# Blocks 4 to 7 of x: turned by DMA and VectorE instead of TensorE in the first pass of a graph layer

## The chip, the cores and the metric

The kernel runs on one core of one Trainium2 chip, in float32. The metric is the device time of one execution in microseconds; lower is better. Times within a profile are microseconds from the start of its span. TensorE (PE, with its weight loads PEld), VectorE (DVE), ScalarE (ACT), GpSimd (POOL) and SyncE (SP, which here issues most DMAs) each work through their own instructions in order.

## The reference

One layer on x of 4096 rows by 256, with a weighted adjacency of 4096 by 4096:

```python
def _layernorm(x, axis=-1, eps=1e-5):
    m = jnp.mean(x, axis=axis, keepdims=True)
    v = jnp.var(x, axis=axis, keepdims=True)
    return (x - m) / jnp.sqrt(v + eps)
...
    def _L0_gnn_ref(features, adj, neigh_W, lin_W):
        h = features @ neigh_W.T
        deg = adj.sum(axis=1, keepdims=True) + 1.0
        h = adj @ h / deg
        z = jnp.concatenate([features, h], axis=-1) @ lin_W.T
        return z
...
    x = x + _L0_gnn_ref(_layernorm(x, axis=-1), adj, L0_gnn_neigh_W, L0_gnn_lin_W)
    x = x + _L0_ffn_ref((_layernorm(x, axis=-1))[None], ...)[0]
```

The second half, causal attention over the 4096 rows and eight experts of which each row takes two, comes after all that is spoken of here.

## The kernel before

x is held as 8 blocks of 512 rows, `res[b]`, each of 4 tiles of 128 rows. The graph half is `adj` times the normed x (`g`), pass by pass: `aggregate(b, steps)` makes the rows of block b and runs over jb = 0 to 7, the blocks of neighbours. One (b, jb) is called a step. It takes seven products of half-size matrices (a Strassen-like scheme, L538) from the adjacency block `a` (1 MB, three buffers, loaded by SyncE three steps ahead at the end of each step, L278), from sums of its quarters, and from the normed block `g[jb]` and its differences. The sums are made by `halve(n)` on VectorE (L495 to L498).

The program is written under a manual schedule: each engine's instructions run in the order in which the code issues them. Work is put in by hand: after the fourth product of a step, the functions in `steps[jb]` are issued; after the seventh those of `steps[jb, "end"]`; then `load(...)`; then `steps[jb, "loaded"]`.

The first pass (b = 0) also prepares x, in functions that take a block:

- `scales_x`: mean and variance on VectorE (`bn_stats` L159, `bn_aggr` L161), then rstd on GpSimd in two operations (L165, L166).
- `normed_x`: VectorE norms a tile into `g[b]` (L451); the four of block b+1 are issued at the head of `features(b)`.
- `turned_x`: TensorE turns the normed block, 8 transposes of 128x128 (L437), and ScalarE copies them out of PSUM into `qT[b % 4]` (L439).
- `features`: TensorE multiplies the turned block by the first half of lin_W, 8 matmuls (L509), and VectorE adds the result onto `res[b]` (L514).
- `halve_x`: a small copy of ones into a column of `g[b]` (ScalarE, L463; that column gives the degrees), then VectorE makes four differences (L467 to L470), which read the ones.

In step jb the list is halve(jb+1), features(jb+2), halve_x(jb+2), scales_x(jb+4), and at its end turned_x(jb+3). Blocks 0 and 1 are done ahead of the first step, and turned_x(2) in step 0. In step 3 `load_rest` issues the loads of the attention's weights.

In the later passes `qkv(b - 1)` puts the projections of the block finished before into the steps. It has another way to turn a block: `norm` puts the normed rows, in an order of columns grouped by 32, into `kT[b]` and `vv[b]` (not yet used for their own ends); `leave` stores these in a DRAM tile `turning` (L599, two DMAs); `fetch` brings them back so that every 32x32 square lies where it belongs (L611, four DMAs, runs of 256 bytes); `turn` turns the squares on VectorE (L621, two instructions).

Of the kernel before, what the change touches and what calls it, by code (L numbers as in the profile page):

```python
# [9 lines left out]
F32 = mybir.dt.float32  # L10
I32 = mybir.dt.int32
SP = mybir.EngineType.SP
AF = mybir.ActivationFunctionType
ALU = mybir.AluOpType
# [3 lines left out]
P = 128  # L18
N = 4096
C = 256  # L20
NB = 8
TB = 4
# [9 lines left out]
Q = HD // 2  # L32
# [34 lines left out]
def fast_kernel(  # L67
# [24 lines left out]
    nc = tc.nc  # L92
# [13 lines left out]
    ones = const.tile([P, P], F32, name="ones")  # L106
# [13 lines left out]
    for e in range(NE):  # L120
# [16 lines left out]
    res = [  # L137
        res_all[:, b * TB * C : (b + 1) * TB * C].rearrange("p (t c) -> p t c", t=TB)
        for b in range(NB)
    ]  # L140
    qT_all = const.tile([P, NB * 2 * 512], F32, name="qT_all")
# [4 lines left out]
    mv = [const.tile([P, TB, 2], F32, name=f"mv{b}") for b in range(NB)]  # L146
# [42 lines left out]
    def in_order(x):  # L189
        return x.rearrange("p (g c d) -> p c g d", g=4, c=2)  # L190

    def in_groups(x):
        return x.rearrange("p (c g d) -> p c g d", g=4, c=2)
# [65 lines left out]
    with (  # L259
# [161 lines left out]
        HC = C // 2  # L421
# [17 lines left out]
                nc.scalar.copy(dst[:, :, cols], tr.rearrange("p c t i -> p c (t i)"))  # L439

        turned = {}

        def scales_x(b, at_a_time=TB):
            for t in range(0, TB, at_a_time):
                some = slice(t, t + at_a_time)
                stats(gx, b, range(TB)[some])
                power(rstd[b][:, some], mv[b][:, some, 1:2], 1.0, EPS_LN)

        def normed_x(b, t):
# [3 lines left out]
                mv[b][:, t, 0:1], rstd[b][:, t], op0=ALU.subtract, op1=ALU.mult,  # L453
            )

        def turned_x(b):

            turned[b] = qT[b % 4]
            transposed(lambda t, c: g[b][:, t // 2 * 2 + c, t % 2, :], turned[b])

        def halve_x(b):

            nc.scalar.copy(  # L463
                g[b][:, 1:4:2, :, HC - 1], ones[:, 0:4].rearrange("p (k t) -> p k t", k=2)
            )
            part = [g[b][:, k] for k in range(7)]
            nc.vector.tensor_sub(part[T1], part[G12], part[G11])  # L467
            nc.vector.tensor_sub(part[T3], part[G22], part[G12])
            nc.vector.tensor_sub(part[T2], part[G22], part[T1])
            nc.vector.tensor_sub(part[T4], part[T2], part[G21])  # L470
# [28 lines left out]
            halves_of[n] = m  # L499
        def features(b):  # L500
            fT = turned.pop(b)
            for t in range(TB if b + 1 < NB else 0):
                normed_x(b + 1, t)
            for h in range(2):
                pj = p_pj.tile([P, 2, C], F32, tag="pj", name=f"pf_{b}_{h}")
                for t in range(2):
                    for c in range(2):
                        at = (2 * h + t) * P
                        nc.tensor.matmul(  # L509
                            pj[:, t, :], fT[:, c, at : at + P], l1_sb[:, c, :],  # L510
                            start=(c == 0), stop=(c == 1),
                        )
                x1 = res[b][:, 2 * h : 2 * h + 2, :]
                nc.vector.tensor_add(x1, x1, pj)  # L514
# [52 lines left out]
                ),  # L567
            )

        turning = [tc.dram_tile([512, C], F32, name=f"turning{n}") for n in range(2)]  # L570
        last_z = gs.tile([P, 1024], F32, name="last_z")

        def qkv(b):

            made = {}

            def scales():
                stats(gx, b)
                var = mv[b][:, :, 1:2]
                power(both[b], var, *BOTH)  # L580
                power(rstd[b], var, 1.0, EPS_LN)

            def norm():

                made["h0"] = [
                    t.rearrange("p (t c) -> p t c", t=2)
                    for t in (kT[b], vv[b].rearrange("p t c -> p (t c)"))
                ]
                for t in range(TB):
                    nc.vector.tensor_scalar(  # L590
                        in_order(made["h0"][t // 2][:, t % 2, :]), in_groups(res[b][:, t, :]),
                        mv[b][:, t, 0:1], both[b][:, t], op0=ALU.subtract, op1=ALU.mult,
                    )
                made["ratio"] = ratio(gx, b)

            def leave():

                for n, h0 in enumerate(made.pop("h0")):
                    nc.sync.dma_start(  # L599
                        turning[b % 2][n * 2 * P : (n + 1) * 2 * P].rearrange(  # L600
                            "(t p) c -> p t c", p=P
                        ),
                        h0,
                    )

            def fetch():

                made["z"] = qT_all[:, (b + 1) * 1024 : (b + 2) * 1024] if b + 2 < NB else last_z
                squares = turning[b % 2].rearrange("(m i) (g e) -> g i m e", i=Q, g=4)
                for n in range(4):  # L610
                    nc.sync.dma_start(  # L611
                        made["z"][n * Q : (n + 1) * Q].rearrange("p (m e) -> p m e", e=2 * Q),
                        squares[n],
                    )

            def turn():

                made["hT"] = qT[b]
                z = made.pop("z").rearrange("p (m c d) -> p c m d", c=2, d=Q)
                for c in range(2):  # L620
                    nc.vector.transpose(  # L621
                        qT[b][:, c, :].rearrange("p (m i) -> p m i", i=Q), z[:, c]
                    )

            def values_and_logits():
                for h in range(2):
                    pj = p_tr.tile([P, 2, 2, P], F32, tag="tr", name=f"pv_{b}_{h}")
                    pj = pj.rearrange("p c t i -> p c (t i)")
                    for i in range(2):
                        at = (2 * h + i) * P  # L630
                        for c in range(2):
                            nc.tensor.matmul(  # L632
                                pj[:, i, 0 : NE + P], made["hT"][:, c, at : at + P],
                                wqkv_sb[:, c, QK:], start=(c == 0), stop=(c == 1),
                            )
                    nc.scalar.copy(vv[b][:, 2 * h : 2 * h + 2, :], pj[:, :, NE : NE + P])  # L636
                    for i in range(2):
                        t = 2 * h + i
                        nc.scalar.activation(
                            first_lg[b][:, t, :], pj[:, i, 0:NE], AF.Copy,  # L640
                            scale=made["ratio"][:, t],
                        )

            def turned_heads(ms):
                pjs = [p_pj.tile([P, 512], F32, tag="pj", name=f"pq_{b}_{m}") for m in ms]
                for m, pj in zip(ms, pjs):
                    for c in range(2):
                        nc.tensor.matmul(
                            pj, wqkv_sb[:, c, m * P : (m + 1) * P], made["hT"][:, c, :],
                            start=(c == 0), stop=(c == 1),  # L650
                        )
                for m, pj in zip(ms, pjs):
                    to = kT[b] if m == 2 else qT[b][:, m, :]
                    rot = gx.tile([P, 512], F32, tag="rot", name=f"rot_{b}_{m}", bufs=1)
                    nc.vector.tensor_mul(to, pj, tables[b][:, 0, :])  # L655
                    for n in range(4):
                        nc.scalar.activation(  # L657
                            rot[n * Q : (n + 1) * Q, :], pj[(n ^ 1) * Q : ((n ^ 1) + 1) * Q, :],
                            AF.Copy, scale=1.0 if n % 2 else -1.0,
                        )  # L660
                    nc.gpsimd.tensor_mul(rot, rot, tables[b][:, 1, :])  # L661
                    nc.gpsimd.tensor_add(to, to, rot)

            return [
                [scales, lambda: turn_tables(b)], [norm, leave], [],
                [values_and_logits, lambda: turned_heads((2,))], [lambda: turned_heads((0, 1))],
            ], {
                (2, "end"): [fetch], (2, "loaded"): [lambda: spread_tables(b)],
                (3, "end"): [turn],
            }  # L670
# [26 lines left out]
        steps = {jb: [] for jb in range(NB)}  # L697
        for jb in range(NB):
            for f, b in (
                (halve, jb + 1), (features, jb + 2), (halve_x, jb + 2), (scales_x, jb + 4),  # L700
            ):
                if b < NB or f is halve:
                    steps[jb].append(lambda f=f, b=b: f(b))
            if jb + 3 < NB:
                steps[jb, "end"] = [lambda b=jb + 3: turned_x(b)]
        steps[0].insert(1, lambda: turned_x(2))
        steps[3].append(load_rest)
        for jb, f in ((5, scale_rest), (6, bounds), (6, turn_wo), (7, router_wo)):
# [2117 lines left out]
```

## Time and profile before

| | us |
|---|---|
| median of 3 runs | 1512.12 (1512.09 to 1512.35) |
| the profiled execution, its own time | 1511.47 |
| its span, first to last instruction | 1509.8 |
| ahead of the first step | 0 to 18.46 |
| first pass, step 0 | 18.46 to 30.41 |
| steps 1 to 4, each | 10.37 or 10.38 |
| step 5 | 71.90 to 81.28 |

| instruction (mean in the first pass) | ns |
|---|---|
| transpose on TensorE, record, 128x128 (L437) | 276 |
| copy of 128x512 out of PSUM on ScalarE (L439) | 588 |
| norm of a tile of 128x256 on VectorE (L451) | 408 |
| `bn_stats` of a tile (L159) | 412 |
| square transposes of 128x512 on VectorE (L621) | 691 |
| copy of ones on ScalarE (L463) | 209 |

A line of the order of time gives start, length, engine and line of the kernel, operation, output and input, how many were merged, and in brackets for how long the engine was idle before it and what ended that. A line of the busy times by stage gives the stretch, its length, then for PE, PEld, DVE, ACT and POOL busy microseconds and instructions, then the granted TensorE clock (1 is full), the share of the DMA engines and GB/s. Records of matmuls overlap, so a group's cost is read from starts, not from the sum of records.

### The profile page before, as it was taken

How to read it: one execution, taken by the hardware profiler on the slowest of the kernel's cores; microseconds unless marked ns; L12 is line 12 of the kernel's file. 1: busy time of each engine (PE TensorE's matmuls, PEld its weight loads, DVE VectorE, ACT ScalarE, POOL GpSimd, SP SyncE). 2: the span in 40 equal slices, each digit the busy share in tenths (PEclk: the TensorE clock that was granted, in tenths of full speed). 3: DMA queues.
4: the chain of work that ended last, by engine and by line, in shares of the span. 5: the costliest groups of instructions: out<-in, count | busy, mean ns of one | idle time of the engine just before them, and what ended most of it. 6: DMA issues, size and time to landing. Idle time of an engine off the chain costs nothing. (4 is left out here: it accounts for less than half of the span.)

```text
span 1509.8 us, 28585 instructions
## 1 busy us (share of the span) xinstructions
PE 1496.9 (99%) x10731; PEld 1102.8 (73%) x10731; DVE 1083.9 (72%) x2239; ACT 544.9 (36%) x975; POOL 568.9 (38%) x649
## 2 busy tenths in 40 slices
PE   9999999999999999999999999999999999999997
PEld 7888888888888544444444444358899999999996
DVE  7855666656765577779879879795676877777872
ACT  2102011021020455655665655653222334343341
POOL 2102122121221331374565553551523464554542
PEclk9999999999999999999999999999999999999999
DMA  7435645555566000011010110029977898999965
GB/s 244 133 119 178 201 147 173 166 170 171 162 184 185 21 15 22 24 59 30 30 59 28 36 41 30 30 87 336 251 180 225 254 278 233 264 272 246 270 155 135
DMA packets 127005, 220.56 MB, mean 146 GB/s; under 512 B 79530, under 2 KB 103338, under 8 KB 113226
## 3 DMA queue, kind: packets, MB, share of 16 engines
q1 hardware_dynamic: 113322, 200.39, 42.3%
q0 software_dynamic: 12720, 17.47, 6.6%
q8 instruction: 86, 1.41, 0.4%
q10 hardware_dynamic: 816, 0.79, 0.2%
q14 instruction: 61, 0.50, 0.1%
HBM read 188.67 MB, written 31.33 MB: 146 GB/s over the span
## 5 line engine op out<-in xcount | busy, mean ns | idle before, releaser
L826 PE MATMUL sc<-qT_all,kT 64*64 64x512 f32 (+3 forms) x2304 | 282.1, 557 | 0.5 <-ACT pt_all L834 0.3
L538 PE MATMUL acc<-a,g 128*128 128x256 f32 x1024 | 244.0, 379 | 0.0
L538 PEld LDWEIGHTS acc<-a,g 128*128 128x128 f32 x1024 | 194.1, 190 | 32.2 <-issue 6.7
L826 PEld LDWEIGHTS sc<-qT_all,kT 64*64 64x64 f32 x2304 | 91.3, 133 | 128.9 <-issue 109.9
L834 ACT ACTIVATE pt_all<-sc 128x1024 f32<-128x1024 f32 (+3 forms) x157 | 149.0, 956 | 99.9 <-PE sc L826 95.6
L1917 POOL DMA_INDIRECT acc_dram<-y,late x40 | 63.3, 1583 | 177.0 <-ACT y L1906 118.9
L538 PE MATMUL acc<-more_sums,g 128*128 128x256 f32 x512 | 126.3, 379 | 0.0
L854 DVE TENSOR_TENSOR late<-late,pt_all 128x1024 f32<-128x1024 f32 (+3 forms) x92 | 106.6, 1159 | 20.4 <-ACT pt_all L834 9.0
L661 POOL TENSOR_TENSOR rot<-rot,tables 128x512 f32<-128x512 f32 x21 | 34.4, 1636 | 192.4 <-ACT rot L657 137.3
L538 PEld LDWEIGHTS acc<-more_sums,g 128*128 128x128 f32 x512 | 97.2, 190 | 13.2
L868 PE MATMUL y_second<-pt_all,vv 64*64 64x512 f32 (+3 forms) x440 | 105.0, 555 | 0.0
L868 PE MATMUL y_first<-pt_all,vv 64*64 64x512 f32 (+3 forms) x440 | 104.3, 553 | 0.0
L1837 PE MATMUL h<-late,qT_all 128*128 128x256 f32 (+1 forms) x616 | 104.0, 327 | 0.0
L1837 PEld LDWEIGHTS h<-late,qT_all 128*128 128x128 f32 x616 | 93.5, 191 | 9.6 <-ACT late L1521 0.8
L1110 POOL DMA_INDIRECT lists<-row,slots x64 | 91.3, 1426 | 17.2 <-issue 14.5
L636 ACT COPY vv<-pv 128x256 f32<-128x256 f32 x14 | 5.2, 373 | 251.9 <-PE pv L632 216.0
L868 PE MATMUL y_third<-pt_all,vv 64*64 64x512 f32 (+3 forms) x376 | 89.8, 557 | 0.0
L1844 DVE TENSOR_TENSOR late<-si,h 128x256 f32<-128x256 f32 (+2 forms) x87 | 39.3, 466 | 64.4 <-ACT si L1843 44.6
L657 ACT ACTIVATE rot<-pq 32x512 f32<-32x512 f32 x84 | 49.5, 589 | 82.5 <-DVE qT_all L655 33.1
L1843 ACT ACTIVATE si<-h 128x256 f32<-128x256 f32 (+2 forms) x87 | 36.1, 418 | 107.0 <-PE h L1837 93.1
L538 PE MATMUL acc<-qT_all,g 128*128 128x256 f32 x256 | 65.7, 379 | 0.0
L854 DVE TENSOR_TENSOR sum_all<-sum_all,pt_all 128x1024 f32<-128x1024 f32 (+3 forms) x49 | 53.5, 1093 | 15.8 <-POOL pt_all L836 9.9
(480 smaller groups left out, 3321.4 us busy)
## 6 DMA issues: line engine op xcount, KB each, us to landing
a<-in_adj_dram SPq DMA_DIRECT2D x64, 1024.0 KB
qT_all<-in_w_dram SPq DMA_DIRECT2D x18, 1408.0 KB
pt_all<-in_w_dram SPq DMA_DIRECT2D x16, 1408.0 KB
res_all<-in_w_dram SPq DMA_DIRECT2D x17, 768.0 KB
pt_all<-in_w_dram SPq DMA_DIRECT2D x16, 768.0 KB
res_all<-in_w_dram SPq DMA_DIRECT2D x8, 1408.0 KB
qT_all<-in_w_dram SPq DMA_DIRECT2D x9, 768.0 KB
late<-lists SPq DMA_DIRECT2D x96, 64.0 KB
```

Source lines behind the costliest of these rows:

```text
L538: nc.tensor.matmul(acc[bank][:, at, :], g[jb][:, right, k, :], m[left][:, k, :], start=(jb == 0 and k == 0 and at == 0), stop=(jb == NB - ...
L657: nc.scalar.activation(rot[n * Q : (n + 1) * Q, :], pj[(n ^ 1) * Q : ((n ^ 1) + 1) * Q, :], AF.Copy, scale=1.0 if n % 2 else -1.0,)
L661: nc.gpsimd.tensor_mul(rot, rot, tables[b][:, 1, :])
L826: nc.tensor.matmul(ps[k * HP : (k + 1) * HP, j, :w], kT[sb][hd, i * P + k * HP : i * P + (k + 1) * HP], qT[b][hd, p, off:], start=True, st ...
L834: nc.scalar.activation(pt[:, :, :w], ps[:, :, :w], AF.Exp, scale=HD ** -0.5)
L854: nc.vector.tensor_add(sums[b, p][:, :, off:], before[:, :, off:], pt[:, :, : 512 - off])
L868: nc.tensor.matmul(accs[b, p][k][hd, off:], vv[sb][some, i, hd], pt[some, j, : 512 - off], start=(s == order_of(b)[0]), stop=(s == order_o ...
L1110: put = nc.gpsimd.indirect_dma_start(out=lists[:, :], out_offset=bass.IndirectOffsetOnAxis(ap=chosen[b][:, k, t, :], axis=0), in_=flats[b] ...
L1837: nc.tensor.matmul(ps[m % 2][:, m // 2 - q, :], w13_sb[:, c, m * P : (m + 1) * P], xT[:, c, :], start=(c == 0), stop=(c == 1),)
L1843: nc.scalar.activation(si[:, 0:both, :], ps[0][:, 0:both, :], AF.Silu)
L1844: nc.vector.tensor_mul(hT[:, q : q + both, :], si[:, 0:both, :], ps[1][:, 0:both, :])
L1917: put = nc.gpsimd.indirect_dma_start(out=(acc_dram if k < NM - LAST else out)[:, :], out_offset=at, in_=y[:, h, :], in_offset=None, comput ...
```

## The change

For blocks 4 to 7 (`FIRST = 4`) the way of `qkv` replaces `normed_x` and `turned_x`. ScalarE norms each tile twice, as scale and bias (`staged_x`): into the staging tiles `kT[b]` and `vv[b]`, then into `g[b]`. GpSimd first makes the bias, minus mean times rstd (`less`, a tile with one buffer). SyncE stores the staging tiles (`left`) and fetches the squares (`fetched`), VectorE turns them (`squares_x`). In steps 1 to 3 `scales_x` and `staged_x` of block jb+4 are issued ahead of `halve(jb+1)`; those of block 4 in and at the end of step 0, its store after that step's load. The store of block jb+4 stands at the end of step jb, the fetch of block jb+3 at the end of the list of step jb (1 to 4), its square transposes at that step's end. For blocks 4 to 7 the ones of `halve_x` are copied by GpSimd. The helpers are the old ones of `qkv`, which now calls them too.

```diff
         turned = {}
+        turning = [tc.dram_tile([512, C], F32, name=f"turning{n}") for n in range(2)]
+
+        def rows_of(b):
+            return [
+                t.rearrange("p (t c) -> p t c", t=2)
+                for t in (kT[b], vv[b].rearrange("p t c -> p (t c)"))
+            ]
+
+        def left(b):
+            for n, rows in enumerate(rows_of(b)):
+                nc.sync.dma_start(
+                    turning[b % 2][n * 2 * P : (n + 1) * 2 * P].rearrange(
+                        "(t p) c -> p t c", p=P
+                    ),
+                    rows,
+                )
+
+        def fetched(b, z):
+            squares = turning[b % 2].rearrange("(m i) (g e) -> g i m e", i=Q, g=4)
+            for n in range(4):
+                nc.sync.dma_start(
+                    z[n * Q : (n + 1) * Q].rearrange("p (m e) -> p m e", e=2 * Q), squares[n]
+                )
+
+        def turn_squares(z, dst):
+            z = z.rearrange("p (m c d) -> p c m d", c=2, d=Q)
+            for c in range(2):
+                nc.vector.transpose(dst[:, c, :].rearrange("p (m i) -> p m i", i=Q), z[:, c])
...
+        FIRST = 4
+
+        def staged_x(b):
+
+            less = gx.tile([P, TB, 1], F32, tag="less", name=f"less_{b}", bufs=1)
+            nc.gpsimd.tensor_scalar(
+                less, mv[b][:, :, 0:1], -1.0, 0.0, op0=ALU.mult, op1=ALU.add
+            )
+            nc.gpsimd.tensor_mul(less, less, rstd[b])
+            staged = rows_of(b)
+            for t in range(TB):
+                nc.scalar.activation(
+                    in_order(staged[t // 2][:, t % 2, :]), in_groups(res[b][:, t, :]),
+                    AF.Identity, bias=less[:, t], scale=rstd[b][:, t],
+                )
+            for t in range(TB):
+                i = t // 2 * 2
+                nc.scalar.activation(
+                    g[b][:, i : i + 2, t % 2, :],
+                    res[b][:, t, :].rearrange("p (h c) -> p h c", h=2),
+                    AF.Identity, bias=less[:, t], scale=rstd[b][:, t],
+                )
+
+        def fetched_x(b):
+            fetched(b, z_of(b))
+
+        def squares_x(b):
+            turned[b] = qT[b % 4]
+            turn_squares(z_of(b), turned[b])
+
+        def z_of(b):
+            return qT_all[:, (4 + b % 2) * 1024 : (5 + b % 2) * 1024]
...
-            nc.scalar.copy(
-                g[b][:, 1:4:2, :, HC - 1], ones[:, 0:4].rearrange("p (k t) -> p k t", k=2)
-            )
+            ones_at, four = g[b][:, 1:4:2, :, HC - 1], ones[:, 0:4].rearrange(
+                "p (k t) -> p k t", k=2
+            )
+            if b < FIRST:
+                nc.scalar.copy(ones_at, four)
+            else:
+                nc.gpsimd.tensor_copy(ones_at, four)
...
-            for t in range(TB if b + 1 < NB else 0):
+            for t in range(TB if b + 1 < FIRST else 0):
                 normed_x(b + 1, t)
...
             for f, b in (
-                (halve, jb + 1), (features, jb + 2), (halve_x, jb + 2), (scales_x, jb + 4),
+                (scales_x, jb + 4), (staged_x, jb + 4), (halve, jb + 1), (features, jb + 2),
+                (halve_x, jb + 2),
             ):
-                if b < NB or f is halve:
+                if jb and b < NB or f is halve:
                     steps[jb].append(lambda f=f, b=b: f(b))
+            if not jb:
+                steps[0] += [
+                    lambda: features(2), lambda: halve_x(2), lambda: scales_x(4),
+                ]
+            if FIRST <= jb + 3 < NB:
+                steps[jb].append(lambda b=jb + 3: fetched_x(b))
             if jb + 3 < NB:
-                steps[jb, "end"] = [lambda b=jb + 3: turned_x(b)]
+                steps[jb, "end"] = [
+                    lambda f=turned_x if jb + 3 < FIRST else squares_x, b=jb + 3: f(b)
+                ]
+            if not jb:
+                steps[0, "end"].append(lambda: staged_x(4))
+            if jb + 4 < NB:
+                steps[jb, "loaded" if not jb else "end"] = steps.get(
+                    (jb, "loaded" if not jb else "end"), []
+                ) + [lambda b=jb + 4: left(b)]
         steps[0].insert(1, lambda: turned_x(2))
```

More of the change, by code (lines that the diff above doesn't have):

```diff
@@ L568, in turn_banks @@
             )
-        turning = [tc.dram_tile([512, C], F32, name=f"turning{n}") for n in range(2)]
         last_z = gs.tile([P, 1024], F32, name="last_z")
@@ L583, in norm @@
             def norm():
[L585 to L588, printed above, removed]
+                h0 = rows_of(b)
                 for t in range(TB):
                     nc.vector.tensor_scalar(
-                        in_order(made["h0"][t // 2][:, t % 2, :]), in_groups(res[b][:, t, :]),
+                        in_order(h0[t // 2][:, t % 2, :]), in_groups(res[b][:, t, :]),
                         mv[b][:, t, 0:1], both[b][:, t], op0=ALU.subtract, op1=ALU.mult,
@@ L596, in leave @@
             def leave():
[L598 to L603, printed above, removed]
-                    )
+                left(b)
             def fetch():
                 made["z"] = qT_all[:, (b + 1) * 1024 : (b + 2) * 1024] if b + 2 < NB else last_z
[L609 to L614, printed above, removed]
+                fetched(b, made["z"])
             def turn():
                 made["hT"] = qT[b]
[L619 to L623, printed above, removed]
+                turn_squares(made.pop("z"), qT[b])
             def values_and_logits():
```

## The prediction, made before the changed kernel was run

> **What bounds the kernel now.** I read the page's busy times first, then TensorE's waits, then the stages of the first pass, then each engine's order of time inside them. On the page:
>
> ```profile
> PE 1496.9 (99%) x10731; PEld 1102.8 (73%) x10731; DVE 1083.9 (72%) x2239; ACT 544.9 (36%) x975; POOL 568.9 (38%) x649
> ```
>
> TensorE is busy 99% of the span, and in its list of waits no line before the experts reaches 1.5 us. So a microsecond of TensorE's work that goes is a microsecond gained, and a microsecond for which it is made to wait is one lost; I work with TensorE's clock alone. Busy time by stage, five columns of engines, the granted clock behind them (steps jb = 1 to 5 of the first pass):
>
> ```profile
> 30.41:40.78 10.37, 10.37 (x54) 9.19 (x53) 10.13 (x27) 1.06 (x4) 2.00 (x2) 1.00 0.29 101
> 40.78:51.15 10.37, 10.37 (x54) 9.18 (x53) 9.66 (x27) 1.17 (x4) 2.07 (x2) 1.00 0.30 103
> 51.15:61.53 10.38, 10.38 (x55) 9.20 (x54) 8.36 (x23) 1.18 (x4) 2.07 (x2) 1.00 0.58 178
> 61.53:71.90 10.37, 10.37 (x55) 9.18 (x54) 8.24 (x22) 1.17 (x4) 2.07 (x2) 1.00 0.30 103
> 71.90:81.28 9.38, 9.38 (x46) 8.28 (x45) 4.60 (x9) 3.07 (x9) 0.00 (x0) 1.00 0.31 112
> ```
>
> The first four contain the turning of a block (x4 to x7) on TensorE, the fifth none: 10.37 - 9.38 = 0.99 us a block. The third column, VectorE, is what to keep in mind: 10.13 of 10.37 us in step 1. It hardly rests before 47 us, and it is behind. Its order of time and GpSimd's in step 1:
>
> ```profile
> 31.30 0.42 DVE L467 TENSOR_TENSOR g<-g 128x256 f32<-128x256 f32 x1
> ...
> 32.89 1.40 DVE L159 BATCH_NORM_STATS2 st<-res_all 128x6 f32<-128x256 f32 x4
> 34.20 0.36 DVE L161 BATCH_NORM_AGGREGATE mv<-st 128x2 f32<-128x6 f32 x4
> ...
> 34.66 0.54 POOL L165 TENSOR_SCALAR rstd<-mv 128x4 f32<-128x4 f32 x1 [6.22 <-DVE mv L161]
> 35.28 1.45 POOL L166 TENSOR_TENSOR rstd<-rstd,half 128x4 f32<-128x4 f32 x1
> ...
> 39.67 0.42 DVE L467 TENSOR_TENSOR g<-g 128x256 f32<-128x256 f32 x1
> ```
>
> The statistics of block 4 were issued in step 0, yet are made at 32.89, in step 1; rstd is there at 36.73. The subtractions of block 3 (`halve_x(3)`) begin at 39.67. The kernel already has the round trip in its later passes, one block a pass; two lines of SyncE's queue and the transpose that waits (second such trip):
>
> ```profile
> 116.66 1.15 SPq L599 DMA_DIRECT2D turning<-vv  x1
> 119.64 1.92 SPq L611 DMA_DIRECT2D qT_all<-turning  x4
> 182.94 1.31 DVE L621 STREAM_TRANSPOSE qT_all<-qT_all 128x512 f32<-128x512 f32 x2 [4.37 <-DMA qT_all<-turning]
> ```
>
> From the issue of the second store to the first fetch it is 2.33 to 2.35 us in six of the seven trips (2.98 in the first, shown, where the issue itself took long); from the first fetch to the transpose 4.75 to 5.79, middle 5.1.
>
> **What the Trainium skill says.** "ScalarE: Activation LUTs", What ACT_TABLE_LOAD costs: an ACTIVATE takes 186 ns + 0.833 ns an element, 93 ns more for each per-partition operand, and neighbours overlap by 93. The trace agrees where it can: L346, 128x384 with one such operand, 614 ns (599 by the page). For 256 elements with two operands that is an estimate of 585 ns, one every 0.50 us. "DMA: Bandwidth & Descriptors", Anatomy of one DMA: a wait for a semaphore happens on the issuing sequencer. The 2.35 us between store and fetch on SyncE are such a wait, and what is queued behind it waits too. "TensorE: Matmul & The Clock Gate", What's actually happening: after an idle window of about 3.4 us the clock falls to half. Here it was granted whole 2 to 5 us after the last matmul (1500.96) and is half at 6 to 8:
>
> ```profile
> 2.93:4.43 1.50, 1.50 (x10) 1.50 (x9) 0.00 (x0) 0.76 (x1) 0.00 (x0) 1.00 0.93 298
> 4.43:5.93 1.50, 1.50 (x16) 1.43 (x14) 0.97 (x4) 0.72 (x2) 0.02 (x1) 1.00 1.09 374
> 1503.00:1506.00 3.00, 0.00 (x0) 0.00 (x0) 0.00 (x0) 0.00 (x0) 1.12 (x1) 1.00 0.73 88
> 1507.00:1509.00 2.00, 0.00 (x0) 0.00 (x0) 0.00 (x0) 0.00 (x0) 0.00 (x0) 0.50 0.00 0
> ```
>
> The first two rows are the start: 10 transposes in 1.5 us, then 16, some 3 us after the first one; a cold start is slow for about 3 us.
>
> **The change, part by part.**
>
> *TensorE* loses the eight transposes (L437) of blocks 4 to 7: 4 x 0.99 = **-3.96 us**, all on the path.
>
> *ScalarE* loses their copies (8 x 0.588) and four copies of ones (0.21), and gets 32 activations at 0.50 us: 16 us over four steps, against some 1.2 us busy in each. That is hidden as load, not as order (below).
>
> *VectorE* loses 16 norms (L451, 1.38 us a block) and gets two square transposes a block (1.31 us, L621): even. Its statistics move ahead of `halve(jb+1)` by 1.6 us: in step 1, statistics of block 5 at 34.5 to 36.1, `halve(2)` to 38.8. Step 2 begins at 30.41 + 9.38 = 39.79, so this is free, with 1.0 us to spare.
>
> *GpSimd* gets two small operations for `less` a block: 0.54 us (L165's time beside VectorE) and an unknown one; L165 alone has taken 0.19, one VectorE operation it may have to wait for is 0.69. I take 1.2 us for the pair, bounds 0.4 and 1.4; neither can be a gain, since nothing is taken away. The copies of ones for blocks 4 to 7 come here, about 0.2 us.
>
> *SyncE* gets two stores and four fetches a block: 0.75 + 1.92 us of issue, x4 = 10.7 us, and 4.2 MB, in a stage where the DMA share is 0.3. In step 1 they stand ahead of `load(4)`, with two waits: that load goes out about 46 instead of 40.2. A load takes about 5 us (issued 29.74, the DMA engines at rest by 35) and `halve(4)` comes after 55 in the new order: free, covered by three buffers of the adjacency. Loads 5 and 6 have the same room.
>
> *The chain of block 4*, which decides. rstd 36.73; `less` 37.9; ScalarE from 38.0, four activations (two into each staging tile) at 40.1, all eight at 42.1; second store issued 40.2; fetch 42.55 (+2.35); square rows in 47.65 (+5.1); VectorE 1.31: turned at 48.95.
>
> *The wait that the order adds.* ScalarE's copy of ones for block 3 (L463) is issued in step 1 behind all of `staged_x(5)`. That needs `less` of block 5, whose tile has one buffer: free once block 4's eight activations are done, 42.1, so `less` 43.4, activations 43.5 to 47.6, ones 47.8. Queued behind it on VectorE: `halve_x(3)` waits from 40.2 to 47.9, takes 1.67 (39.67 to 41.34 before), and only then, 49.6, come the squares of block 4, to **50.9**, not 48.95.
>
> *Who waits for that.* TensorE comes to `features(4)` after four products of step 2: 39.79 + 3.35 = 43.15 (3.35 from 40.78 to the weights at 44.13 before). It can go on at 51.0: **+7.85 us** of idle TensorE. Bounds: the data's chain alone with `less` at 0.4 and the quickest fetch, 4.75, gives 47.8, so 4.7; `less` at 1.4 in both places gives 8.3.
>
> *The cold clock.* An idle stretch of 7.9 us is longer than the 5 to 6 us after which the clock was half at the end. Restart slow for about 3 us, so **+1.5 us**; bounds 0 (gate not reached) and 3.4 (two of the page's windows at half rate).
>
> *The other blocks.* After 50.9 VectorE needs 1.6 + 2.7 + 1.3 + 1.7 + 1.3 = 8.6 us (statistics, halve, adds, halve_x, squares) to the next squares; TensorE 3.45 + 2.58 + 3.35 = 9.38 to the next features. Block 5's rows are in by 54, its squares at 58.2 at the earliest. So blocks 5 to 7 follow without a stall, by 0.8 us. I take nothing for them; if it fails, up to 1 us in all.
>
> **Sum:** -3.96 + 7.85 + 1.5 = +5.4. The profiled execution took 1511.47 (span 1509.8 and 1.7 around it), so 1516.9 for it; it lies 0.65 below the median 1512.12, on which the forecast stands: **1517.5**.
>
> **Rivals.** Less or more than 0.2% (3.0 us) is about what a measurement here can tell from none.
>
> *A, forecast, chance 0.58:* one stall of 6.5 to 8.5 us at `features(4)` and a cold restart, 1515.5 to 1519.
>
> *B, 0.18:* the stall is the data's chain alone, 4.7 to 6 us, since ScalarE gets to the ones earlier than I have it. For it: the times of `less` are guessed. Against: the order of issue. -3.96 + 5.9 = +1.9, 1514.1; with a cold clock up to 1515.6. Two thirds of it are no change.
>
> *C, ends faster, 0.10:* the round trip closes in time. Place: the statistics of block 4. If VectorE came to them when they are issued rather than some 6 us behind, the chain would hide and all 3.96 us stay: 1508.2. It decides at a wait under 0.94 us at `features(4)`, so rows turned by 44.1. For it: blocks 5 to 7 have that lead. Against: nothing in VectorE's queue ahead of 32.89 changes, and from rstd (36.73) on the quickest parts of the chain add up to 11 us, where 6.4 are left.
>
> *D, 0.14:* the 0.8 us of margin fail, VectorE becomes the bound of steps 2 to 4 and each block adds 1 to 2 us: about 1521.
>
> **Numbers.** Slower: A, D and a third of B, 0.78; same 0.12; faster 0.10. Eight in ten: from 1512.9 (B's low end, 4.7 without a cold clock) to 1521.0 (8.3 and 3.4, or D's middle).
>
> **What would show it.** In the after, TensorE waits for VectorE's square transposes once, at the features of block 4, near 43 us, for 6 to 8 us; VectorE idle before `halve_x(3)`, released by ScalarE's ones; the clock half for some 3 us after; steps of 9.4 us from then on. No wait there of over a microsecond, or statistics of block 4 well before 32.9, proves me wrong.

## The result, and the profile after

| | before | after |
|---|---|---|
| median of 20 runs each | 1512.63 | 1515.05 |
| the profiled execution | 1511.47 | 1514.92 |
| its span | 1509.8 | 1513.2 |

The ratio is 1.0015 with a 95% interval of 1.0008 to 1.0022: slower by 2.4 us. Line numbers of the changed kernel differ: transposes L437, statistics L159, rstd L165 and L166 as before; `less` L489 and L492, activations L495 and L501, stores L452, fetches L462, square transposes L469, ones L528 (ScalarE) and L530 (GpSimd), differences L532 to L535, sums of `halve` L560 to L563, features L574, products L603.

Busy time by stage again, steps 1 to 5 of the first pass (length, PE, PEld, DVE, ACT, POOL, granted clock, DMA share, GB/s):

```profile
30.41:39.79 9.38, 9.38 (x46) 8.28 (x45) 9.17 (x28) 3.88 (x9) 4.11 (x6) 1.00 0.42 141
39.79:56.64 16.85, 12.44 (x45) 10.20 (x44) 9.89 (x25) 8.69 (x20) 3.30 (x7) 0.80 0.81 196
56.64:66.14 9.50, 9.50 (x46) 8.36 (x45) 8.24 (x21) 3.69 (x9) 3.03 (x6) 1.00 0.97 239
66.14:75.63 9.49, 9.49 (x45) 8.36 (x44) 6.59 (x13) 3.08 (x8) 0.19 (x1) 1.00 1.06 245
75.63:85.13 9.50, 9.50 (x45) 8.36 (x44) 6.76 (x13) 0.00 (x0) 0.00 (x0) 1.00 0.31 112
```

Four of the five steps are shorter than or near those of before; step 2 takes 16.85 us, of which TensorE is busy 12.44, at a clock of 0.80. Together 54.72 us where it was 50.87: +3.85 at the end of step 5. TensorE's order of time in that step, and who ends its wait:

```profile
43.03 0.59 PE L603 MATMUL acc<-qT_all,g 128*128 128x256 f32 x2
48.04 2.04 PE L574 MATMUL pf<-qT_all 128*128 128x256 f32 x4 [4.42 <-DVE qT_all L469]
```

One wait of 4.4 us, for VectorE's square transposes, ahead of the features of block 4. From the weights' side it is 43.25 to 48.01, 4.76 us. The features then take until 54.05, 6.04 us where they took 3.45. The stage view cut at the change of the clock says why:

```profile
43.20:46.70 3.50, 0.43 (x2) 0.03 (x1) 1.07 (x3) 2.36 (x6) 0.00 (x0) 1.00 1.12 285
46.70:48.00 1.30, 0.00 (x0) 0.00 (x0) 1.27 (x4) 0.00 (x0) 0.00 (x0) 0.50 1.08 353
48.00:53.50 5.50, 5.46 (x13) 4.41 (x14) 5.22 (x14) 0.38 (x1) 2.91 (x5) 0.50 0.97 173
53.50:56.60 3.10, 3.10 (x16) 2.74 (x15) 2.06 (x5) 3.10 (x8) 0.00 (x0) 1.00 0.43 136
```

The clock falls to half after 3.5 us of rest (from the weights' side) and stays there for 6.8 us, 5.5 of them at work. What VectorE had waited for, with the activations and the ones of ScalarE ahead of it (order of time, two engines):

```profile
36.80 1.09 ACT L495 ACTIVATE kT<-res_all,less,rstd 128x256 f32<-128x256 f32 x2 [5.50 <-POOL less L492]
...
43.42 2.06 ACT L501 ACTIVATE g<-res_all,less,rstd 128x256 f32<-128x256 f32 x4
45.38 0.18 ACT L528 COPY g<-ones 128x4 f32<-128x4 f32 x1
45.60 0.42 DVE L532 TENSOR_TENSOR g<-g 128x256 f32<-128x256 f32 x1 [5.57 <-ACT g L528]
...
47.20 1.30 DVE L469 STREAM_TRANSPOSE qT_all<-qT_all 128x512 f32<-128x512 f32 x2
```

Activations come one every 0.50 us. VectorE rests 5.57 us ahead of `halve_x(3)` until ScalarE has copied the ones; the square transposes follow it without waiting for the rows. So the order of queues ended last, as forecast, but some 2 us earlier.

### The profile page after: what moved, and what is told of

Its sections match the earlier page's. It is cut to its first block, busy times and chain, and to the rows that moved or that the text cites. A ratio compares the mean times of both kernels' runs of the same rounds, so it can differ in the third digit from the quotient of the medians.

```text
span 1513.2 us, 28586 instructions
## 1 busy us (share of the span) xinstructions
PE 1496.8 (99%) x10699; PEld 1101.9 (73%) x10699; DVE 1083.2 (72%) x2231; ACT 555.9 (37%) x995; POOL 566.6 (37%) x661
## 5 line engine op out<-in xcount | busy, mean ns | idle before, releaser
L603 PE MATMUL acc<-a,g 128*128 128x256 f32 x1024 | 243.4, 379 | 0.0
L603 PEld LDWEIGHTS acc<-a,g 128*128 128x128 f32 x1024 | 194.4, 190 | 32.4 <-issue 6.7
L603 PE MATMUL acc<-more_sums,g 128*128 128x256 f32 x512 | 126.3, 379 | 0.0
L603 PEld LDWEIGHTS acc<-more_sums,g 128*128 128x128 f32 x512 | 97.2, 190 | 13.2
L1170 POOL DMA_INDIRECT lists<-row,slots x64 | 89.6, 1400 | 18.2 <-issue 16.1
L603 PE MATMUL acc<-qT_all,g 128*128 128x256 f32 x256 | 65.7, 379 | 0.0
```

The costliest lines, as they stand in the source:

```text
L603: nc.tensor.matmul(acc[bank][:, at, :], g[jb][:, right, k, :], m[left][:, k, :], start=(jb == 0 and k == 0 and at == 0), stop=(jb == NB - ...
L1170: put = nc.gpsimd.indirect_dma_start(out=lists[:, :], out_offset=bass.IndirectOffsetOnAxis(ap=chosen[b][:, k, t, :], axis=0), in_=flats[b] ...
```

## The experiments

Ratios are to the kernel before, run on the same chip. Gains in microseconds are taken from the ratio; the medians of the same runs can differ from that by up to 0.7 us. To say where TensorE stands late in the first pass, I use the start of `p_bounds`, a small product that the function `bounds` issues in step 6. My theory after the result: one wait at one place (the features of block 4), fed by block 4's late statistics and by the ones behind block 5's activations, made dearer by the clock. The rivals: the rows' way alone; slow features for a reason other than the clock; VectorE as bound of the whole pass.

**The ones of block 3 on GpSimd.**

```diff
-            if b < FIRST:
+            if b < 3:
                 nc.scalar.copy(ones_at, four)
```

> Only the ones of block 3 move from ScalarE's queue (behind the eight activations of block 5) to GpSimd's. If the order of the ones sets the end of the wait, halve_x(3) starts at about 41.5 instead of 45.6, the squares of block 4 start when their rows land, 46.2 (fetch 41.1 + 5.1), and TensorE waits about 3.8 us instead of 4.8 at the features of block 4. An idle stretch of 3.8 us is so near the 3.5 us after which the clock fell in the changed kernel that it may fall or not: 1514.0 with a cold restart, about 1511.7 without. Rival: the rows themselves come at 47.2, and the ones only happened to be ready then; then nothing changes, 1515.0.

Measured: 1514.12, ratio 1.0010 (1.0004 to 1.0017). VectorE's order of time:

```profile
41.66 0.42 DVE L532 TENSOR_TENSOR g<-g 128x256 f32<-128x256 f32 x1 [1.55 <-POOL g L530]
...
46.20 1.31 DVE L469 STREAM_TRANSPOSE qT_all<-qT_all 128x512 f32<-128x512 f32 x2 [2.85 <-DMA qT_all<-turning]
```

The differences come 3.9 us sooner, the transposes 1.0 us sooner, and what they wait for is now the DMA: the ones were last by 1.0 us, the rows next. The features start at 47.05. In this profile the clock stayed whole through a rest of 3.7 us from the weights' side (3.3 between products), longer than the 3.5 after which it had fallen in the changed kernel. Of 21 executions 15 had a granted clock of 0.997 or less, where 69 of 73 of the kernel before have 0.998 or 0.999, so most seem to have had a slow stretch still. The time is that of the first of the two cases expected, but that the clock makes it is not shown: the profiled execution, with a whole clock and `p_bounds` at 85.3 (85.1 before), took 1515.47, and TensorE waits 2.8 us in it for the experts' weights.

**A filler for TensorE while it waits.**

```diff
+        FILL = 36
...
             fT = turned.pop(b)
+            if b == FIRST:
+                filler = p_tr.tile([P, 2, 2, P], F32, tag="tr", name="filler")
+                for n in range(FILL):
+                    nc.tensor.transpose(filler[:, n % 2, n // 2 % 2, :], ident, ident)
```

> 36 transposes of the identity into a free PSUM bank ahead of the features of block 4, some 4.5 us of work for TensorE in the stretch in which it only waits (their results are not used). Theory: the clock stays whole, the features take 3.45 us instead of 6.0, and the time falls by about 2.5 us to 1512.6 although TensorE waits for the same rows. Rival: the features are slow for another reason (rows or weights that come late), then 1515 or, with the added work, more.

Measured: 1514.24, ratio 1.0018 (1.0011 to 1.0024). TensorE:

```profile
43.56 4.09 PE L571 MATMUL filler<-ident 128*128 128x128 f32 x36
48.16 3.79 PE L579 MATMUL pf<-qT_all 128*128 128x256 f32 x16 [0.50 <-DVE qT_all L469]
51.79 1.03 PE L608 MATMUL acc<-a,g 128*128 128x256 f32 x4
```

The features start as late as in the changed kernel, but the clock stays whole: it is 3.63 us from the start of the features to that of the products, where the changed kernel took 6.23, and `p_bounds` comes 2.5 us sooner (86.4 instead of 88.9). That the slow features were the clock's is shown. That it is worth 2.5 us of the whole is not: the ratio is that of the changed kernel within its interval, so the time that was expected, 1512.6, was missed. The profile has one new wait, 1.3 us at the start of the experts, for their weights.

**Three blocks instead of four.** FIRST = 5, no `staged_x(4)`; the norms of block 4 on VectorE in step 1 behind the statistics of block 5, the ones of blocks 3 and up on GpSimd.

```diff
-        FIRST = 4
+        FIRST = 5
...
-            if not jb:
-                steps[0, "end"].append(lambda: staged_x(4))
-            if jb + 4 < NB:
+            if jb and jb + 4 < NB:
...
+        steps[1].insert(2, lambda: [normed_x(4, t) for t in range(TB)])
```

> Block 4 goes back to TensorE's transposes and VectorE's norms; blocks 5 to 7 keep the way through DRAM; ones of blocks 3 and up on GpSimd. Theory: the wait is block 4's alone, since only there are the statistics late. No wait at any features, no cold clock, and three blocks x 0.89 us (3.55 us by four blocks in the changed kernel's steps) are gained: 1512.6 - 2.7 = 1509.9. Rival: the wait moves to block 5, the first to go through DRAM: then 2 to 5 us at the features of block 5, 1512 to 1516. Rival: VectorE bounds the first pass and nothing is gained, 1512.6.

Measured: 1509.32, ratio 0.9979 (0.9973 to 0.9986), 3.2 us faster than before (2.6 by the medians). TensorE's list of waits in the first pass (18 to 100 us) is one line, which the kernel before also has:

```profile
PE pf L574 <- ACT qT_all L439: 0.2, 1, 0.2
```

`p_bounds` is at 82.4 instead of 85.1: 2.7 us for three blocks, 0.9 each. Both rivals fall: the wait did not move to block 5, and VectorE did not bound the pass.

**The statistics of block 5 back behind `halve`.**

```diff
-                (scales_x, jb + 4), (staged_x, jb + 4), (halve, jb + 1), (features, jb + 2),
+                (halve, jb + 1), (scales_x, jb + 4), (staged_x, jb + 4), (features, jb + 2),
```

> The statistics of block 5 (and 6, 7) go back behind halve, as in the kernel before; all else as in the changed kernel. GpSimd's work for block 4 then runs beside halve's sums of two operands and not beside bn_stats. Theory: its two operations for rstd take 0.54 and 1.45 us again (0.19 and 1.01 in the changed kernel), and as the statistics of block 5 come 2.7 us later, so do its rows and the ones of block 3 that are queued behind them: features of block 4 start at 49 to 50 instead of 48.0, so 1516 to 1517. Rival: GpSimd is as quick as in the changed kernel whatever VectorE does, and only block 5's activations wait: 48.5, 1515.5.

Measured: 1516.41 in 6 executions, ratio 1.0029 (1.0017 to 1.0041). GpSimd and VectorE in the changed kernel, and in this one:

```profile
34.48 1.37 DVE L159 BATCH_NORM_STATS2 st<-res_all 128x6 f32<-128x256 f32 x4
34.65 0.19 POOL L165 TENSOR_SCALAR rstd<-mv 128x4 f32<-128x4 f32 x1 [6.22 <-DVE mv L161]
34.93 1.01 POOL L166 TENSOR_TENSOR rstd<-rstd,half 128x4 f32<-128x4 f32 x1
```

```profile
34.51 0.54 POOL L165 TENSOR_SCALAR rstd<-mv 128x4 f32<-128x4 f32 x1 [6.22 <-DVE mv L161]
35.03 0.69 DVE L561 TENSOR_TENSOR qT_all<-qT_all,a 128x512 f32<-128x512 f32 x1
35.13 1.45 POOL L166 TENSOR_TENSOR rstd<-rstd,half 128x4 f32<-128x4 f32 x1
35.82 0.69 DVE L562 TENSOR_TENSOR more_sums<-a,qT_all 128x512 f32<-128x512 f32 x1
...
36.57 0.60 POOL L489 TENSOR_SCALAR less<-mv 128x4 f32<-128x4 f32 x1
```

The same operations on the same data take 0.79 us longer beside the sums of `halve`, which read two operands, than beside `bn_stats`, which reads one. TensorE's wait grows from 4.4 to 5.3 us. So the theory holds for GpSimd. The delay that follows is smaller than expected: the features start at 48.7, not at 49 to 50, as block 5's `less` starts only 0.7 us later (41.62 instead of 40.93); it waited for its buffer, not for its statistics.

**The statistics of block 4 ahead of VectorE's adds of features(2).** The ones of block 3 go to GpSimd here too. `features` now takes a function that it calls ahead of its own products and adds.

```diff
-        def features(b):
+        def features(b, between=lambda: None):
             fT = turned.pop(b)
             for t in range(TB if b + 1 < FIRST else 0):
                 normed_x(b + 1, t)
+            between()
...
-                    lambda: features(2), lambda: halve_x(2), lambda: scales_x(4),
+                    lambda: features(2, lambda: scales_x(4)), lambda: halve_x(2),
```

> The ones of block 3 on GpSimd, and the statistics of block 4 issued ahead of VectorE's adds of features(2) and halve_x(2), so at 30.1 instead of 32.9. Theory: all of block 4's chain comes 2.8 us sooner: TensorE waits 1 to 2 us at its features instead of 4.8, too short for the clock to fall. 1512.6 - 3.55 + 1.5 = 1510.5. Rival: adds and differences that come later hold TensorE in their turn, or the rows' way is the same whenever it starts: 1513 to 1515.

Measured: 1509.52, ratio 0.9981 (0.9975 to 0.9988), 2.9 us faster than before (2.4 by the medians), with all four blocks through DRAM. Statistics at 30.16, square transposes at 43.09:

```profile
30.16 1.40 DVE L159 BATCH_NORM_STATS2 st<-res_all 128x6 f32<-128x256 f32 x4
...
43.09 1.30 DVE L469 STREAM_TRANSPOSE qT_all<-qT_all 128x512 f32<-128x512 f32 x2 [1.42 <-DMA qT_all<-turning]
...
43.95 2.28 PE L575 MATMUL pf<-qT_all 128*128 128x256 f32 x9 [0.26 <-DVE qT_all L469]
```

Statistics that start 2.7 us sooner, with the 1.0 us of the ones, took 4.2 us out of the wait (4.42 to 0.26), and no other wait appears in the first pass.

**Features and square transposes one step later.** Features of block b in step b-1 for the four blocks, the square transposes in the step before, the ones of block 3 ahead of `staged_x(4)`.

```diff
-                (scales_x, jb + 4), (staged_x, jb + 4), (halve, jb + 1), (features, jb + 2),
-                (halve_x, jb + 2),
+                (scales_x, jb + 4), (staged_x, jb + 4), (halve, jb + 1),
+                (squares_x, jb + 2), (features, jb + 1 if jb > 2 else jb + 2),
+                (halve_x, jb + 2),
             ):
+                if f is squares_x and jb < 2 or f is features and jb == 2:
+                    continue
```

> The square transposes and the features of blocks 4 to 7 one step later (features of block b in step b-1), the ones of block 3 ahead of block 4's activations on ScalarE. The features are not needed before the end of the pass. Theory: the whole loss was one wait at one place, so with all four blocks through DRAM no features wait and the four turnings are gained in full: 0.89 x 4 = 3.55 us, 1508.4 beside a kernel before at 1512.0. Rival: a step without features is 5.9 us, shorter than VectorE's work for it, so halve of block 3 comes late and TensorE waits there for 1 to 3 us: 1509.5 to 1511.5.

Measured: 1510.46, ratio 0.9986 (0.9977 to 0.9994), 2.1 us faster. No features wait for rows and no halve comes late, but there is a new wait:

```profile
78.05 3.62 PE L581 MATMUL pf<-qT_all 128*128 128x256 f32 x16
83.39 0.92 PE L356 MATMUL p_bounds<-wqkv_sb 128*64 128x64 f32 x24 [1.72 <-issue]
```

`bounds` in step 6 takes a PSUM bank of the same two as the features of block 7, now issued just ahead of it; VectorE begins to add those up at 82.61, and TensorE goes on as the first add ends.

**The same, with `bounds` and `turn_wo` (which turns weights of the attention) at the end of step 6.**

> The kernel with late features, and bounds and turn_wo at the end of step 6 instead of behind features(7) in its middle. In the run with late features TensorE waited 2.1 us ahead of p_bounds, whose PSUM bank the features of block 7 had just filled and VectorE, three instructions behind, had not yet added up. Theory: with three products between, that wait goes, and the first pass is shorter by all of 4 x 0.89 us: 3.5 us below the kernel before. Rival: the bank was not the reason, and 1.7 to 2.1 us are again waited for there: 1.5 us below the kernel before.

Measured: 1509.59, ratio 0.9977 (0.9966 to 0.9987), 3.5 us faster, though with an interval of 2.0 to 5.1. The wait at `p_bounds` is gone once three products stand between, which fits the bank as its cause. But the full 3.5 us are not in the profile: at `p_wo`, a product of step 7, TensorE is 2.8 us ahead of the kernel before (89.6 instead of 92.4), since the features of block 5 wait 0.7 us for VectorE (weights' side). This kernel, the one with three blocks and the one with early statistics lie within each other's intervals; each beats both given kernels.

**TensorE delayed alone.** The kernel before with 12 such transposes at the features of block 4.

> The kernel before with 12 transposes of the identity (results not used) ahead of the features of block 4: TensorE comes out of the first pass some 1.3 us later, with no wait and a whole clock, as it did in the run with the filler. Theory: a shift of TensorE alone is passed on one to one, 1512.0 + 1.3 = 1513.3, and the extra microsecond of the filler run (a wait for the experts' weights of 1.3 us in its profile) is not the shift's doing. Rival: the shift by itself brings that wait, since the loads of the experts' weights have no room: 1514.3 or more.

Measured: 1512.96, ratio 1.0006 (0.9997 to 1.0014): `p_bounds` at 86.3 instead of 85.1, and 0.4 us slower than a before of 1512.61 there by medians, 0.9 by the ratio (its interval is -0.5 to 2.1 us). So a delay of 1.2 us shows no further microsecond of its own; the 2.3 us of the rival lie just outside the interval. Its profile has a wait of 0.5 us for the experts' weights.

**The ones on GpSimd, and a filler of 26 transposes.**

> The ones of block 3 on GpSimd (features of block 4 at 47.0, as measured with that edit alone) and 26 transposes of the identity, 3.2 us, in the stretch in which TensorE waits. Theory: the wait of 3.5 us without a cold clock costs about what the four turnings gained: the kernel before within 0.5 us; with the edit of the ones alone it was 1.0010 of it, part of its executions with a slow clock. Rival: the clock is of no account for the whole time, 1.0010 again.

Measured: 1514.22, ratio 1.0009 (1.0001 to 1.0018). The clock was 0.998 or 0.999 in all 13 executions, the features start at 47.6, `p_bounds` at 85.8: 0.7 us late, near the 0.5 expected. The whole is 1.3 us late, and again the profile has a wait for the experts' weights:

```profile
PE h L1902 <- DMA qT_all<-in_w_dram: 1.6, 1, 1.6
```

A miss, of the same kind as with the first filler.

**The changed kernel again.**

> The changed kernel itself, beside the other two on the same chip: 1.0015 of the kernel before by all theories, 2.4 us above it, most executions with a granted clock of 0.996[...] where the kernel before has 0.998 to 0.999.

Measured: 1515.37, ratio 1.0015 (1.0008 to 1.0022), as the first time; 10 of 21 executions at a clock of 0.996 or 0.995 (I expected most), 7 at 0.997, 4 at 0.998. In this profile the clock fell after 4.2 us of rest, 0.7 later than in the first one, and stayed at half for 6.8 us again. Its executions at 0.996 have a median of 1515.81, those at 0.998 of 1514.94.

## Why the prediction was right, and where it was not

Forecast 1517.5 (1512.9 to 1521.0), slower with 0.78; measured 1515.05. The direction, the place and the order of the queues were right; the sum was too large by 1.5 us in the first pass. The time is inside the range, but below the forecast A's own (1515.5 to 1519), and the wait of 4.8 us is outside A's 6.5 to 8.5. The slowdown, 0.16% by the medians, is also less than the 0.2% that I had set as the least to be told from none; with 20 executions of each kernel the interval (0.08 to 0.22%) leaves out zero. That the sum came this near is in part luck: the wait was 3.1 us less than forecast, while the cold clock cost 1.1 more and the turnings gave 0.5 less.

| term | forecast | profile after |
|---|---|---|
| TensorE's turnings | -3.96 | -3.50 |
| wait at the features of block 4 | +7.85 | +4.76 |
| cold clock | +1.5 | +2.59 |
| first pass, sum | +5.4 | +3.85 |
| the whole, profiled execution | +5.4 | +3.45 |

- *TensorE's turnings.* I compared a step with a turning to step 5, 9.38 us. Step 5 follows a turning, and its first products start 0.1 us sooner for it; later steps without one take 9.50. So 0.88 a block, not 0.99. Three blocks through DRAM gained 2.7 in the first pass, which agrees.
- *The wait,* the term that was mis-sized most, 3.1 us. The step that failed is GpSimd's, in "The chain of block 4, which decides". It took rstd at 36.73 from a trace in which VectorE was then at `halve`. The prediction itself had moved the statistics of block 5 to that very time, and did not carry it over. rstd was there at 35.94; `less` took 0.86 us where I had 1.2, so block 4's activations began at 36.80 instead of 38.0. They ended at 40.84, the second `less` took 0.5 us instead of 1.2, and the ones came at 45.56 instead of 47.8. The run with the statistics back behind `halve` shows the cause of 0.8 us of these 2.2, that of rstd. Most of the others are the two `less`, priced at 1.2 us each within bounds of 0.4 and 1.4; the second took 0.5 us in that run as well. Another 0.6 us: TensorE starts on the first of the two square transposes, I waited for both. Of the rest, 0.2 us, half is that TensorE stopped at 43.25 instead of 43.15.
- *The order of the ones.* Right: the ones were last, with 1.0 us, half of what I had between the two ends (50.9 and 48.95).
- *The rows' way.* Right: store to fetch 2.22 us (2.35 forecast). In the changed kernel the fetch's end is hidden by the ones; where the transposes waited for it, fetch to transposes took 5.0 us with the ones on GpSimd and 4.9 with the early statistics (5.1 forecast).
- *The cold clock.* Right in kind. The clock fell after 3.5 us of rest, not after 5 to 6, and stayed low for 5.5 us of work, not 3. The Trainium skill, "TensorE: Matmul & The Clock Gate", What's actually happening, has windows of 3.4 us that run on whatever the kernel does; the prediction used their length and not that. The 6.8 us at half are as long as two of them, and such windows would explain why the clock fell after 3.5, 3.7 and 4.2 us in three profiles and not after 3.7 in a fourth. My bound of 3.4 us from that page held.
- *The other blocks.* Right: no other features wait. VectorE reached block 5's square transposes 9.84 us after block 4's (8.6 forecast), since TensorE was slow and its adds came late; the rows, forecast to be in by 54, came at 57.0, with no time to spare (0.29 us waited). That no later features waited was thus nearer than the forecast had it.
- *The rivals.* C fell at the place it named: statistics at 32.89 in the changed kernel too. Starting them at 30.16 made it true, with the ones moved: a wait of 0.26 us. B was nearer than A: the wait was of its size (4.7 to 6), the time below its upper end with a cold clock (1515.6), and what it gave for itself, that `less` was guessed and ScalarE would come to the ones earlier, held. Only its claim that the data's chain alone sets the wait did not: the ones were still last, by 1.0 us. D did not happen.

Of the +3.85 us of the first pass the profiled execution kept 3.45 and the medians 2.4. Between these two, the profiled execution of the kernel before lies 1.2 us below its median of 20, that of the changed kernel 0.1 below its own. Also, the clock seems not to fall, or to fall for less time, in some executions: 11 of 20 had 0.996 (median 1515.25), 4 had 0.998 (1513.9). The rest I cannot place. The kernels with a filler, whose first pass is 1.3 and 0.7 us late, are 2.3 and 1.3 us late in the whole by the medians, and their profiles have waits for the experts' weights (1.3 and 1.6 us; the run with the ones alone 2.8). Such waits are not theirs alone, though: the last of the fast kernels has 1.1 us of it in its profile, the delay alone 0.5. What sets those weights' landing, and whether it is what these kernels lose, stays open.

## What to carry to other kernels

A step moved to an engine with time to spare is hidden only if its chain, head to tail, fits between the moment its first input is really made and the moment its result is due: here that was 6 us for a chain of 11, because VectorE made the statistics in the step after the one that issued them. Look for what is queued behind the moved work on its new engine: a 0.2 us copy of ones, eight activations deep, set the end. And when a rest of TensorE grows past some 3.5 us, count on a slow stretch after it. Leaving one block on the old way, or issuing 1.6 us of statistics sooner, each with the ones moved too, turned a loss of 2.4 us into a gain of about 3.

## What the runs showed of the hardware

- GpSimd's small operations on 128x4 depend on what VectorE does beside them: 0.19 and 1.01 us beside `bn_stats`, 0.54 and 1.45 beside sums of two operands, and 0.19 and 1.01 again beside adds of which one operand lies in PSUM (block 5's rstd in the run with its statistics later, at 38.80). The Trainium skill, "GPSIMD Engine Reference", Specifications, says that GpSimd shares its SBUF interfaces with VectorE and contends with instructions that have two SBUF inputs; the numbers agree.
- The clock: from the last weights' load on, it fell to half after 3.5 and 4.2 us of rest in two profiles of the changed kernel and after 3.7 in the run with the statistics later, yet it stayed whole through 3.7 us with the ones on GpSimd. So the length of a rest alone does not decide. Where it fell, it stayed at half for 6.8 us, of which 4.9 to 6.2 were work.
- Fetches of 0.5 MB in runs of 256 bytes took 4.8 to 5.8 us from first issue to use in the kernel before, where a load of 1 MB was issued just behind them, and 9.2 for block 5 in the changed kernel (47.87 to 57.04), whose fetch was issued 3.7 us behind such a load.
